# A two-layer graph attention kernel: the order of its first loads, and the second attention of a group done in two halves

## The chip, the cores and the metric

The kernel runs on one core of a Trainium2 chip. Its engines work in parallel, each through its own queue of instructions in order: TensorE (PE; its weight loads are listed apart, as PEld) multiplies, VectorE (DVE) and ScalarE (ACT) do elementwise work and empty TensorE's result banks (PSUM), GpSimd (POOL) does elementwise work on the on-chip memory (SBUF), and SyncE (SP) issues most of the transfers (DMA). ScalarE and GpSimd can issue transfers too. The metric is the time of one execution on the device in microseconds, lower is better.

## The reference

x is 128 graphs of 64 nodes with 512 features, float32; adj is one 64x64 adjacency matrix shared by all graphs. The layer is computed as

```python
h = relu(layernorm(x))                                 # no scale, no shift
# GAT with 4 heads (W_heads: 4 x 512 x 512, a_heads: 4 x 1024), then ELU
Wh = einsum('bnf,hfo->bhno', h, W_heads)
f1, f2 = Wh . a[:, :512], Wh . a[:, 512:]
e = leaky_relu(f1[..., :, None] + f2[..., None, :], 0.01)
attn = softmax(where(adj > 0, e, -1e9), -1)
h1 = elu(attn @ Wh)  # heads side by side: B x N x 2048
# the same once more, with one head: W_out 2048 x 512, a_out
out = elu(gat(h1, W_out, a_out))                       # the "second attention"
y = relu(out @ w1 + b1) @ w2 + b2 + out
result = x + layernorm(y) * gamma + beta
```

ELU is max(v, exp(min(v, 0)) - 1), written below as an exponential on ScalarE and one instruction on VectorE.

## The kernel before

The 8192 rows are 64 tiles of 128 rows (two graphs each), worked in 16 groups of four tiles. Most matrix products are done by a Strassen-like scheme with seven block products in place of eight (`unit`): the products are numbered p = 1 to 7, and go in the order 1, 5, 6, 2, 3, 7, 4. Between them VectorE and ScalarE add blocks in PSUM. The names in the profile: g_a is the first layer's product (x side to heads), g_b the product with W_out, g_c and g_d the two feed-forward products, pa the second attention, hw and pu the first group's own way of doing the first layer.

The front: the loads, and the first products. `ar` holds a_heads in 8 rows of 512; `spread_a` spreads a row of it over all partitions by a product with the identity; `fold` multiplies the weights by it.

```python
X[0] = load(0)                                     # on SyncE's queue
ar = wk.tile([P, O], FP, tag="elu", name="ar", bufs=3)
nc.vector.memset(ar, 0.0)
nc.sync.dma_start(out=ar[0:2 * H], in_=a_heads.rearrange("h (r p) -> (h r) p", p=O))
for t in range(1, G):
    X[t] = load(t)
# ... cut ...
def fetch(m, after=None):
    MT[m] = big.tile([P, KC, O], FP, tag=homes[m], name=f"pw{m}")
    queue = nc.scalar if m == 0 else nc.sync if m < H else nc.gpsimd
    ins = queue.dma_start(out=MT[m], in_=mats[m].rearrange("(k p) o -> p k o", p=P))
    if after is not None:
        behind(ins, after, "not in front of what is needed first")
    return ins
# ... cut ...
for m in range(H):
    fetch(m)
nc.vector.memset(wa, 0.0)
norm1(0)
ab = spread_a(0)                                   # the first products of TensorE (pab)
transpose_h(0)
# ... cut ...
head_w(0, 1)                                       # eight products (hw) and a copy on ScalarE
transpose_h(2)
fold(3, spread_a(3, LAST["pe"]))
weight_sums(1, LAST["nb"])
weight_sums(2, LAST["nb"])
head_w(0, 2)
transpose_h(3)                                     # four transposes (pth), a copy to hT on ScalarE
head_w(0, 3)                                       # needs hT of tile 3
```

The end of a group's first layer. p = 7's result goes through `post`, whose last instruction in PSUM is the addition on line 607; p = 4, which is put off to the next head's second step (`late`), adds into the bank that this addition reads:

```python
def post(what, a, b=None, to=None):                # in project1: g_a
    # ... cut ...
    if b is not None:
        nc.vector.tensor_tensor(to, a, b, ALU.add) # L607
        a = to
    elu(flat(dst), flat(a), f"{what}_{g}_{h}")
# ... cut ...
return [
    s[0], lambda: (s[1](), flush_late()), lambda: (s[2](), next_sums()), s[3], s[4],
    lambda: (s[5](), late.append(s[6])),
]
```

The second attention, and where it stands among the steps of the next group's first layer (four heads of six steps, numbered 0 to 23; the list `stage_e` is spread evenly over them):

```python
def elu(dst, src, name, on_vector=False):
    ex = wk.tile([P, 512], FP, tag="elu", name=f"ex{name}", bufs=3)
    if on_vector:
        nc.vector.tensor_scalar(ex, src, 0.0, None, ALU.min)       # L572
        nc.scalar.activation(ex, ex, AF.Exp)                       # L573
    else:
        nc.scalar.activation(ex, src, AF.Relu, scale=-1.0)         # L575
        nc.scalar.activation(ex, ex, AF.Exp, scale=-1.0)           # L576
    nc.vector.scalar_tensor_tensor(dst, ex, -1.0, src, ALU.add, ALU.max)   # L577

def attend2_all(g):                                # both halves at once, four PSUM banks
    OUT[g] = big.tile([P, G, FO], FP, tag="out", name=f"o{g}")
    pa = [[aux([P, FO], f"pa2_{g}_0_{b}") for b in range(NB)]]
    pa.append([flat(bank(f"pa2_{g}_1_{b}")) for b in range(NB)])
    for finish in [second_attention(g, q, pa[q]) for q in range(2)]:
        finish()

def stage_e(g):
    gap = [lambda: None]
    score = [lambda j=j: scores2(g, j) for j in range(G)]
    return (
        gap + score + [lambda: spread2(g)] + gap * 2 + [lambda: softmax2(g)] + gap * 5
        + [lambda: transpose_weights2(g)] + gap * 5 + [lambda: attend2_all(g)] + gap * 3
    )
```

`aux` gives one of two auxiliary PSUM banks, `bank` one of the six that the block products use. The order of instructions on an engine is the program's, except that a unit's `post` is given priority and instructions that aren't ready may be passed by others when the program is built.

Of the kernel before, what the change touches and what calls it, by code (L numbers as in the profile page):

```python
# [9 lines left out]
FP = mybir.dt.float32  # L10
AF = mybir.ActivationFunctionType
ALU = mybir.AluOpType
# [10 lines left out]
def gat_preln_kernel(  # L23
# [30 lines left out]
    nc = tc.nc  # L54
    P = 128
# [24 lines left out]
    def bank(name):  # L80
        return ps.tile([P, 2, T], FP, tag="mm", name=name)

    def flat(ap):
        return ap.rearrange("p a b -> p (a b)")
# [8 lines left out]
    def aux(shape, name):  # L93
        return ps.tile(shape, FP, tag="aux", name=name, bufs=2)
# [15 lines left out]
    X[0] = load(0)  # L110

    ar = wk.tile([P, O], FP, tag="elu", name="ar", bufs=3)
    nc.vector.memset(ar, 0.0)
    nc.sync.dma_start(out=ar[0:2 * H], in_=a_heads.rearrange("h (r p) -> (h r) p", p=O))
    for t in range(1, G):
        X[t] = load(t)
    aj = const.tile([P, N], mybir.dt.int32, name="aj")
# [45 lines left out]
# [8 lines that stand above are left out]
    def spread_a(m, after=None):  # L171

        ab = []
        for c in range(2):
            pb = flat(bank(f"pab{m}_{c}"))
            r = 2 * m + c
            ins = nc.tensor.matmul(pb, ident[:, r:r + 1].to_broadcast([P, P]), ar, start=True, stop=True)
            if after is not None:
                behind(ins, after, "not in front of it")
            ab.append(pb)  # L180
        return ab

    def fold(m, ab):

        for c in range(2):
            for k in range(KC):
                junk = wk.tile([P, O], FP, tag="t", name=f"jk{c}_{m}_{k}")
                LAST["fold"] = nc.vector.scalar_tensor_tensor(
                    junk, MT[m][:, k, :], 1.0, ab[c], ALU.mult, ALU.mult,
                    accum_out=wa[:, k, c * H + m:c * H + m + 1],  # L190
                )
# [373 lines left out]

    H1, ZSUM = {}, {}

    def elu(dst, src, name, on_vector=False):

        ex = wk.tile([P, 512], FP, tag="elu", name=f"ex{name}", bufs=3)  # L570
        if on_vector:
            nc.vector.tensor_scalar(ex, src, 0.0, None, ALU.min)  # L572
            nc.scalar.activation(ex, ex, AF.Exp)  # L573
        else:
            nc.scalar.activation(ex, src, AF.Relu, scale=-1.0)  # L575
            nc.scalar.activation(ex, ex, AF.Exp, scale=-1.0)  # L576
        nc.vector.scalar_tensor_tensor(dst, ex, -1.0, src, ALU.add, ALU.max)  # L577

    def quadrant(what):
# [130 lines left out]
    def scores2(g, j):  # L710
        if j == 0:
            F2[g] = sm.tile([P, 2, G], FP, tag="f2", name=f"f2_{g}")
        f = F2[g]
        for c in range(2):
            junk = wk.tile([P, FO], FP, tag="elu", name=f"jf{g}_{j}_{c}", bufs=3)
            nc.vector.scalar_tensor_tensor(  # L716
                junk, WH2[g][:, j], 1.0, ao[:, c, :], ALU.mult, ALU.mult,
                accum_out=f[:, c, j:j + 1],
            )
# [20 lines left out]
    def transpose_weights2(g):  # L740
        A = A2.pop(g)
        pt = aux([P, G, P], f"s2pt{g}")
        for j in range(G):
            nc.tensor.transpose(pt[:, j, :], A[:, j].rearrange("p b m -> p (b m)"), ident)
        AT2[g] = wk.tile([P, G, P], FP, tag="hT", name=f"at2_{g}", bufs=4)
        nc.scalar.copy(AT2[g], pt)

    def attend2(g, q):


        if q == 0:
            tag = "out" if g < NG - 1 else "z11"
            OUT[g] = big.tile([P, G, FO], FP, tag=tag, name=f"o{g}")
        second_attention(g, q, [aux([P, FO], f"pa2_{g}_{q}_{b}") for b in range(NB)])()

    def attend2_all(g):

        OUT[g] = big.tile([P, G, FO], FP, tag="out", name=f"o{g}")
        pa = [[aux([P, FO], f"pa2_{g}_0_{b}") for b in range(NB)]]
        pa.append([flat(bank(f"pa2_{g}_1_{b}")) for b in range(NB)])  # L760
        for finish in [second_attention(g, q, pa[q]) for q in range(2)]:
            finish()

    def second_attention(g, q, pa):
        for b in range(NB):
            rows = slice(b * N, (b + 1) * N)
            for c in range(2):
                nc.tensor.matmul(
                    pa[b][c * N:(c + 1) * N], AT2[g][rows, 2 * q + c, rows],
                    WH2[g][rows, 2 * q + c, :], start=True, stop=True, skip_group_check=True,  # L770
                )

        def finish():
            for b in range(NB):
                elu(OUT[g][:, 2 * q + b], pa[b], f"2_{g}_{q}_{b}", b == 1)
        return finish

    def stage_e(g):

        gap = [lambda: None]  # L780
        score = [lambda j=j: scores2(g, j) for j in range(G)]
        return (
            gap + score + [lambda: spread2(g)] + gap * 2 + [lambda: softmax2(g)] + gap * 5
            + [lambda: transpose_weights2(g)] + gap * 5 + [lambda: attend2_all(g)] + gap * 3
        )


# [82 lines left out]


    for m in range(H):
        fetch(m)
    nc.vector.memset(wa, 0.0)
    norm1(0)
    ab = spread_a(0)
# [14 lines left out]
    head_w(0, 1)  # L891
    transpose_h(2)
    fold(3, spread_a(3, LAST["pe"]))
    weight_sums(1, LAST["nb"])
    weight_sums(2, LAST["nb"])
    head_w(0, 2)
    transpose_h(3)
    head_w(0, 3)
    masks()
    head_w(1, 0)  # L900
# [60 lines left out]
    for g in range(NG):  # L961
        if g >= 1:
            side = stage_e(g - 1)
            done, n = 0, 6 * H
            for i in range(n):
                if i % 6 == 0:
                    steps = project1(g, i // 6)
                steps[i % 6]()
                while done * n < (i + 1) * len(side):
                    side[done]()  # L970
                    done += 1
            flush_late()
        attn = attend1(g + 1) if g + 1 < NG else []
        norms, scores, turns = stage_a(g + 2)
        tr, ff, fin = feed_forward(g - 1) if g >= 1 else ([], [], [])
        if g == NG - 1:
            run(project2(g), tr + [nothing] * 6 + ff[:2])
            run(ff[2:], [
                lambda: [scores2(g, j) for j in range(G)], lambda: spread2(g), nothing, nothing,
                lambda: softmax2(g), *[nothing] * 7, lambda: transpose_weights2(g), nothing,  # L980
                *[lambda q=q: attend2(g, q) for q in range(2)], nothing,
            ])
            continue
        early = [lambda: z_sums(g + 1, 0)] if g else []
        first = mix(attn, tr, [nothing] * len(attn))
        if g >= 1:
            first[5:5] = norms[:1]
            first[10:10] = norms[1:]
        if g == 0:
            side = {  # L990
                0: lambda: (attend0(2, 1), turn0(1, 1), project_f(1)),
                1: lambda: (attend0(3, 1), turn0(2, 1)),
                2: lambda: (turn0(3, 1), scores1(1), attn_weights(2), attn_weights(3)),
                5: lambda: weight_sums(M1, LAST["pe"]),
                7: turns1[1],
                8: lambda: fetch(M2, LAST["pe"]),
                9: attn[0],
                10: lambda: (attn[1](), norms[0](), turns1[4]()),
                12: attn[2],
                13: lambda: (attn[3](), norms[1]()),  # L1000
                15: scores[0],
                16: scores[1],
                17: lambda: weight_sums(M2, LAST["pe"]),
                18: scores[3],
                20: scores[5],
                21: scores[7],
                22: lambda: z_sums(g + 1, 0),
                24: turns[1],
                27: lambda: (turns[4](), load_rows()),
            }  # L1010
            for i, fn in enumerate(project2(g)):
                fn()
                side.get(i, nothing)()
        else:
            run(project2(g), first + mix(
                ff[:7] + early + ff[7:12] + fin[:1] + ff[12:13] + fin[1:2] + ff[13:],
                scores + [nothing] * 8,
            ) + mix(fin[2:], [nothing] + turns + [nothing] * 2))
# [32 lines left out]
```

## Time and profile before

| | before |
|---|---|
| time, median of 3 | 2303.92 us (2303.06 to 2304.11) |
| profiled span | 2302.3 us |
| TensorE busy | 2273.8 us, 99% |
| first TensorE instruction | 6.4 us |
| period of a group, from 304.21 to 444.74 us | 140.53 us |
| granted TensorE clock | 0.998 of full speed |

A line of the timeline is: start in us, duration in us, engine, line of the kernel, operation, the tile written <- the tiles read, shape, type and the number of instructions merged into it; in square brackets the idle time of the engine before it, and what ended it. SPq and ACTq are the DMA-issuing queues of SyncE and ScalarE. A line of the waits is: who waited <- for whom: the sum in us, how many times, the longest. Ends of products are modelled, and products overlap in the array, so a product's duration says less than the distance between two starts. One float32 product is listed as two instructions.

### The profile page before, as it was taken

Reading aid. Unit: us, or ns where it says so; the run is one execution under the profiler, and the core shown is the slowest. Engines: PE = TensorE matmul, PEld = TensorE weight load, DVE = VectorE, ACT = ScalarE, POOL = GpSimd, SP = SyncE. Lnnn points to the kernel's source line nnn. Section 1 sums busy time; section 2 is a strip of 40 time slices with the busy share of each in tenths; the row PEclk is TensorE's granted clock in tenths of the full one; section 3 lists DMA queues with packets and bytes.
Section 4 is the critical chain, followed back from the end, with each engine's and each line's share of the span. In section 5 each row is a group of like instructions: output and inputs, shape, how many; then the busy total and the mean of one; then the engine's idle time right before and its main releaser. Section 6 shows DMA issues by size and latency. Waiting matters only on the chain.

```text
span 2302.3 us, 33214 instructions
## 1 busy us (share of the span) xinstructions
PE 2273.8 (99%) x11856; PEld 1894.7 (82%) x11856; DVE 1334.8 (58%) x2259; ACT 894.4 (39%) x1601; POOL 1016.8 (44%) x906
## 2 busy tenths in 40 slices
PE   8999999999999999999999999999999999999997
PEld 4688888888888888888888888888888888888885
DVE  7546554755657555565665646565465565744537
ACT  3535344252442525335253342524425254241512
POOL 7653524444254442634435344352444425533323
PEclk9999999999999999999999999999999999999999
DMA  7553454644545455454544545445454454635543
GB/s 279 197 183 128 147 183 129 182 130 145 177 132 184 137 156 158 135 183 133 168 144 142 183 129 182 130 147 183 129 181 131 149 173 132 183 118 174 156 148 97
DMA packets 255012, 361.15 MB, mean 157 GB/s; under 512 B 23768, under 2 KB 143608, under 8 KB 254848
## 3 DMA queue, kind: packets, MB, share of 16 engines
q1 hardware_dynamic: 249584, 340.90, 47.5%
q0 software_dynamic: 4576, 16.81, 2.0%
q8 instruction: 96, 1.57, 0.3%
q10 hardware_dynamic: 688, 1.31, 0.2%
q14 instruction: 68, 0.56, 0.1%
HBM read 331.66 MB, written 27.26 MB: 156 GB/s over the span
## 4 chain that ended last, share of the span: by engine, by line
PE 90%; DVE 4%; ACT 3%; issue 1%; DMA 0%; POOL 0%; DVEq 0%; SPq 0%; POOLq 0%; ACTq 0%
PE g_b L305 32%; PE g_a L289 27%; PE g_c L289 8%; PE g_d L305 8%; PE pz L547 4%; PE hw L633 2%; PE pto L798 1%; PE pzS L547 1%; PE s1pt L485 1%; PE pth L362 1%; ACT exc L576 1%; PE s1pe L405 1%; PE pf L372 1%; ACT exc L575 1%; DVE o L577 1%
## 5 line engine op out<-in xcount | busy, mean ns | idle before, releaser
L305 PE MATMUL g_b<-w,h 128*128 128x256 f32 x2560 | 593.2, 380 | 0.0
L305 PEld LDWEIGHTS g_b<-w,h 128*128 128x128 f32 x2560 | 481.5, 190 | 64.1 <-issue 2.0
L289 PE MATMUL g_a<-z,w 128*128 128x256 f32 x1440 | 345.0, 383 | 4.2 <-DVE g_a L607 4.2
L289 PE MATMUL g_a<-zs_z,w 128*128 128x256 f32 x1440 | 330.4, 379 | 0.0
L289 PEld LDWEIGHTS g_a<-z,w 128*128 128x128 f32 x1440 | 268.9, 190 | 60.9 <-DVE g_a L607 14.9
L289 PEld LDWEIGHTS g_a<-zs_z,w 128*128 128x128 f32 x1440 | 273.9, 190 | 37.0
L305 PE MATMUL g_b<-w,hS 128*128 128x256 f32 x1024 | 238.2, 379 | 0.0
L575 ACT ACTIVATE exc<-g_a 128x512 f32<-128x512 f32 x240 | 142.7, 595 | 180.6 <-DVE g_a L607 123.9
L305 PEld LDWEIGHTS g_b<-w,hS 128*128 128x128 f32 x1024 | 192.2, 190 | 24.8 <-issue 0.2
L611 POOL TENSOR_TENSOR hS<-hS,h 128x512 f32<-128x512 f32 x60 | 79.6, 1327 | 260.3 <-DVE hS L577 260.3
L577 DVE SCALAR_TENSOR_TENSOR h<-exc,g_a 128x512 f32<-128x512 f32 x180 | 123.2, 684 | 107.7 <-ACT exc L576 107.1
L314 POOL TENSOR_TENSOR zs_z<-zS,z 128x512 f32<-128x512 f32 x60 | 82.5, 1375 | 214.5 <-PE g_a L289 211.2
L692 POOL TENSOR_TENSOR h<-hS,h 128x512 f32<-128x512 f32 x64 | 81.6, 1275 | 165.9 <-PE g_b L305 165.7
L576 ACT ACTIVATE exc<-exc 128x512 f32<-128x512 f32 x240 | 151.2, 630 | 7.5
L692 POOL TENSOR_TENSOR h<-h,h 128x512 f32<-128x512 f32 x64 | 86.8, 1365 | 138.6 <-PE g_b L305 138.6
L489 ACT COPY at<-s1pt 128x512 f32<-128x512 f32 x64 | 34.4, 590 | 272.1 <-PE s1pt L485 272.1
L849 POOL TENSOR_TENSOR xr<-xr,bs 128x512 f32<-128x512 f32 x64 | 97.5, 1528 | 77.0 <-DMA xr<-in_x_dram 43.0
L289 PE MATMUL g_c<-ot,w 128*128 128x256 f32 x512 | 122.8, 383 | 1.7 <-DVE ot L808 1.5
L305 PE MATMUL g_d<-w,rt 128*128 128x256 f32 x512 | 121.8, 380 | 2.0 <-DVE o L841 1.0
L716 DVE SCALAR_TENSOR_TENSOR jf<-wh,ao 128x512 f32<-128x512 f32 x128 | 118.7, 963 | 7.8 <-ACT wh L698 7.6
L289 PE MATMUL g_a<-zS,w 128*128 128x256 f32 x480 | 113.4, 379 | 0.0
L315 POOL TENSOR_TENSOR zs_z<-z,zs_z 128x512 f32<-128x512 f32 x60 | 81.5, 1359 | 70.2 <-PE g_a L289 47.6
(166 smaller groups left out, 3572.0 us busy)
## 6 DMA issues: line engine op xcount, KB each, us to landing
w<-tc SPq DMA_DIRECT2D x624, 256.0 KB, 2.7
w<-in_L_gnn_W_out_dram SPq DMA_DIRECT2D x192, 256.0 KB, 2.7
w<-in_L_gnn_W_heads_dram SPq DMA_DIRECT2D x180, 256.0 KB, 3.3
w<-in_L_gnn_w_dram SPq DMA_DIRECT2D x96, 256.0 KB, 2.8
x<-in_x_dram SPq DMA_DIRECT2D x64, 256.0 KB, 4.6
xr<-in_x_dram SPq DMA_DIRECT2D x128, 128.0 KB, 2.7
out_dram<-o SPq DMA_DIRECT2D x126, 128.0 KB, 2.4
tc<-pt POOLq DMA_DIRECT2D x20, 512.0 KB, 4.3
```

The source lines that it names most:

```text
L289: LAST["pe"] = nc.tensor.matmul(bk[:, o, :], w[:, k, ts(o, P)], a[:, k, :], start=start and o == 0 and k == 0, stop=k == 1, skip_group_che ...
L305: LAST["pe"] = nc.tensor.matmul(bk[:, j, :], a[:, k, ts(j, P)], w[:, k, :], start=start and n == 0, stop=i == len(ms) - 1 and k == 1, skip ...
L314: eng.tensor_tensor(s2, s1, a11, ALU.subtract)
L315: eng.tensor_tensor(s4, a12, s2, ALU.subtract)
L547: nc.tensor.matmul(banks[b][:, c, :].rearrange("p (h n) -> p h n", h=H), src[rows, off + c * P:off + (c + 1) * P], at[rows, b], start=True ...
L575: nc.scalar.activation(ex, src, AF.Relu, scale=-1.0)
L576: nc.scalar.activation(ex, ex, AF.Exp, scale=-1.0)
L577: nc.vector.scalar_tensor_tensor(dst, ex, -1.0, src, ALU.add, ALU.max)
L611: nc.gpsimd.tensor_tensor(dst, dst, H1["22"][:, h], ALU.add)
L692: nc.gpsimd.tensor_tensor(dst[:, h], x0[:, h], x1[:, h], ALU.subtract)
L716: nc.vector.scalar_tensor_tensor(junk, WH2[g][:, j], 1.0, ao[:, c, :], ALU.mult, ALU.mult, accum_out=f[:, c, j:j + 1],)
L849: nc.gpsimd.tensor_tensor(xr, xr, bs, ALU.add)
```

## The change

Three edits aim at the front: the small load of ar is issued by ScalarE ahead of the first head's weights, which are held until the memset of ar is done, so that ar isn't queued behind a megabyte; the last tile's h is transposed before the product of tile 2 rather than after it, so that its copy is done when its own product comes; and group 2's attention weights are transposed one step later in group 0's product with W_out. The fourth takes the second attention in two halves again, at two steps of the next group's first layer, with two banks each, and all its exponentials go the same way (two instructions on ScalarE).

```diff
@@ front
-    nc.vector.memset(ar, 0.0)
-    nc.sync.dma_start(out=ar[0:2 * H], in_=a_heads.rearrange("h (r p) -> (h r) p", p=O))
+    zeros = nc.vector.memset(ar, 0.0)
+    nc.scalar.dma_start(out=ar[0:2 * H], in_=a_heads.rearrange("h (r p) -> (h r) p", p=O))
@@ elu
-    def elu(dst, src, name, on_vector=False):
+    def elu(dst, src, name):
-        if on_vector:
-            nc.vector.tensor_scalar(ex, src, 0.0, None, ALU.min)
-            nc.scalar.activation(ex, ex, AF.Exp)
-        else:
-            nc.scalar.activation(ex, src, AF.Relu, scale=-1.0)
-            nc.scalar.activation(ex, ex, AF.Exp, scale=-1.0)
+        nc.scalar.activation(ex, src, AF.Relu, scale=-1.0)
+        nc.scalar.activation(ex, ex, AF.Exp, scale=-1.0)
@@ attend2 (attend2_all and second_attention are removed, the matmuls stay in attend2)
-        second_attention(g, q, [aux([P, FO], f"pa2_{g}_{q}_{b}") for b in range(NB)])()
+        pa = [aux([P, FO], f"pa2_{g}_{q}_{b}") for b in range(NB)]
         # ... the eight matmuls of this half, cut ...
-        def finish():
-            for b in range(NB):
-                elu(OUT[g][:, 2 * q + b], pa[b], f"2_{g}_{q}_{b}", b == 1)
-        return finish
+        for b in range(NB):
+            elu(OUT[g][:, 2 * q + b], pa[b], f"2_{g}_{q}_{b}")
@@ stage_e
+        attend = [lambda q=q: attend2(g, q) for q in range(2)]
-            + [lambda: transpose_weights2(g)] + gap * 5 + [lambda: attend2_all(g)] + gap * 3
+            + [lambda: transpose_weights2(g)] + gap * 2 + attend[0:1] + gap * 2 + attend[1:2] + gap * 4
@@ front
     for m in range(H):
-        fetch(m)
+        fetch(m, zeros if m == 0 else None)
@@ front
     fold(3, spread_a(3, LAST["pe"]))
+    transpose_h(3)
     weight_sums(1, LAST["nb"])
     weight_sums(2, LAST["nb"])
     head_w(0, 2)
-    transpose_h(3)
     head_w(0, 3)
@@ steps of group 0's product with W_out (turns[1]: transposes of group 2's first weights)
-                24: turns[1],
+                25: turns[1],
```

The list of `stage_e` grows from 24 to 25 entries over the same 24 steps, so that two entries fall on the first step and every later one comes a step earlier: the softmax of the second attention at step 7 (before 8), its transposes at 13 (before 14), and the halves of the attention at 16 and 19 (before both at 20).

More of the change, by code (lines that the diff above doesn't have):

```diff
@@ L753, in attend2 @@
             OUT[g] = big.tile([P, G, FO], FP, tag=tag, name=f"o{g}")
-        second_attention(g, q, [aux([P, FO], f"pa2_{g}_{q}_{b}") for b in range(NB)])()
[L756 to L764, printed above, removed]
+        pa = [aux([P, FO], f"pa2_{g}_{q}_{b}") for b in range(NB)]
         for b in range(NB):
```

## The prediction

> **What bounds the kernel now.** I read the page's shares first, then the waits of TensorE alone, then three stretches of the timeline: the front, the end of one group's first product, and the end of the program.
>
> The page, busy time and the chain that ended last:
>
> ```profile
> PE 2273.8 (99%) x11856; PEld 1894.7 (82%) x11856; DVE 1334.8 (58%) x2259; ACT 894.4 (39%) x1601; POOL 1016.8 (44%) x906
> ...
> PE 90%; DVE 4%; ACT 3%; issue 1%; DMA 0%; POOL 0%; DVEq 0%; SPq 0%; POOLq 0%; ACTq 0%
> ```
>
> TensorE is idle for 2302.3 - 2273.8 = 28.5 us. Removing work from ScalarE, VectorE or GpSimd is worth nothing by itself; only an idle TensorE, or time that TensorE loses within its own stream, can be won. The waits of TensorE name the idle time:
>
> ```profile
> PE pab L177 <- DMA ar<-in_L_gnn_a_heads_dram: 6.4, 1, 6.4
> PE g_a L289 <- DVE g_a L607: 4.2, 15, 0.3
> ...
> PE hw L633 <- ACT hT L364: 0.7, 1, 0.7
> PE s1pt L485 <- DVE s1A L443: 0.4, 1, 0.4
> ```
>
> The first, third and fourth lie in the front, which the change edits by name; the second comes once in each of 15 groups. The timeline of the front, DMA issues and the first products:
>
> ```profile
> 0.72 0.39 SPq L107 DMA_DIRECT2D x<-in_x_dram  x1
> 0.72 0.47 ACTq L166 DMA_DIRECT2D pw<-in_L_gnn_W_heads_dram  x1
> ...
> 0.90 0.48 DVE L113 MEMSET ar<- 128x512 f32 x1 [0.90 <-PEq L1037]
> ...
> 1.41 0.36 SPq L114 DMA_DIRECT2D ar<-in_L_gnn_a_heads_dram  x1
> ...
> 6.43 3.75 PE L177 MATMUL pab<-ar,ident 128*128 128x512 f32 x4 [6.43 <-DMA ar<-in_L_gnn_a_heads_dram]
> ```
>
> The 16 KB of ar are issued at 1.41 and land 4.88 us later (chain of waits), behind 1 MB of weights issued at 0.72. The 256 KB of x0, issued at 0.72, had landed at 3.54 (VectorE's first statistics start there). TensorE only, end of the first product of a group, with the second attention (pa) in it:
>
> ```profile
> 625.87 1.89 PE L289 MATMUL g_a<-zs_z,w 128*128 128x256 f32 x8
> 627.69 1.95 PE L768 MATMUL pa<-wh,at 64*64 64x512 f32 x16
> 629.57 1.99 PE L289 MATMUL g_a<-z,w 128*128 128x256 f32 x8
> 631.40 3.62 PE L289 MATMUL g_a<-zs_z,w 128*128 128x256 f32 x16
> 634.85 1.03 PE L305 MATMUL g_b<-w,h 128*128 128x256 f32 x4
> 636.15 2.00 PE L289 MATMUL g_a<-z,w 128*128 128x256 f32 x8 [0.27 <-DVE g_a L607]
> 637.99 1.03 PE L305 MATMUL g_b<-w,h 128*128 128x256 f32 x4
> ```
>
> Only differences of start times count here: elsewhere eight such products take 1.727 us from start to start (3.45 for 16), so four take 0.864.
>
> **What the skill says.** (1) "TensorEngine Tiling (Array Packing)", Key Properties: "Changing tiling mode (not just tile) drains the TensorE". The trace agrees: before pa the eight products take 627.69 - 625.87 = 1.82, after it 631.40 - 629.57 = 1.83, so entering the 64x64 form costs 0.09 and leaving it 0.10 us; the 128x128 transposes of the weights (s2pt) elsewhere leave the neighbours at 1.73. (2) "DMA: Bandwidth & Descriptors", Queues, rings and completion order: each DMA engine takes turns between the queue rows that have work, and a completion mark lands only after every earlier write of that engine, across queues. The 4.88 us for 16 KB fit that. (3) "TensorE: Matmul & The Clock Gate", Part 1: the array starts at half rate until a window of some 3.4 us has been busy. The first four products take 3.75 us and the next four of that shape 1.88, so this slow start moves with the first product and isn't saved.
>
> **The change part by part.**
>
> *a. ar issued by ScalarE ahead of the first weights.* Nothing is removed; the order is changed. ar still waits for the memset that ends at 0.90 + 0.48 = 1.38, so it is issued at about 1.4, now with the 1 MB behind it and only x0 and x1 (SyncE no longer stops for ar) in another queue. x0 took 3.54 - 0.72 = 2.82 us alone with the weights; 16 KB in a queue of their own should take 2.2 to 2.8. Estimate: landing at 4.0, TensorE starts about 2.4 us sooner. The first weights leave about 1.1 us later (0.72 to 1.85) and now share the engines with x1 to x3. At the 380 GB/s that the front moves, 0.77 MB of x and 1.05 MB of weights take 4.8 us after x0, so they land by 8.4. They are needed at 12.46 - 2.4 = 10.1 by the first hw product, and by the fold, whose other input (the first four products) ends at 4.0 + 3.75 = 7.75. So no new wait: -2.4.
>
> *b. Tile 3's h transposed a product sooner.* Transposes of tile 3 start at 27.07 and four take 0.43, so the next product could start at 27.50; it starts at 28.40, after the copies of hw (0.58) and hT (0.59) on ScalarE. With a product of 3.43 us between, the copy is long done. Its two auxiliary banks come free by then (copy of hw(0,1) ends at 22.26, the transposes would start at 23.6). -0.9.
>
> *c. Group 2's weights transposed one step later.* The transposes at 155.90 had their input ready (DVE ends 155.34). The 0.44 us wait is at the second set, at 162.55, at the end of VectorE's softmax, which is not shortened. The step moves eight products from behind the first set to ahead of it. 0.
>
> *d. The second attention split again,* 15 groups (the sixteenth was split already). Split, each half is eight 64x64 products: in the first tail group 2250.01 to 2251.02, 1.01 us, and in the front 60.24 to 61.26 (pu), 1.02. Together 16 take 629.57 - 627.69 = 1.88. So two halves cost 2 x 1.02 - 1.88 = 0.16 more inside, and one more entry and exit, 0.19: +0.35 a group, x 15 = +5.3.
>
> *e. The closing wait.* Between 634.85 and 636.15 four products (0.864) take 1.30, so 0.44 us are lost, and the wait's restart makes the next eight 1.84 in place of 1.73: 0.55 in all. Its cause is a VectorE that is late. The product g_a at 636.15 accumulates into a bank that VectorE's L607 must have read; that L607 starts at 635.41, though its input was ready at 635.05, because four elus of pa (four exponentials, two of them behind a VectorE minimum) run from 628.9 to 633.75 and hold back the elu of the unit's first block (634.20, after ScalarE came free) and the L607 before it (634.81). With the split, the elus belong to steps 16 and 19 of 24, where now they all belong to step 20, so one half comes four steps sooner and the other one; VectorE also drops two minimums of 0.69 us a group, and ScalarE gains two of 0.60. The end of the program shows the same four-eight-four order without elus in its way:
>
> ```profile
> 2275.35 1.03 PE L305 MATMUL g_d<-w,rt 128*128 128x256 f32 x4
> 2276.30 2.00 PE L289 MATMUL g_c<-ot,w 128*128 128x256 f32 x8
> 2278.13 1.03 PE L305 MATMUL g_d<-w,rt 128*128 128x256 f32 x4
> ```
>
> Four take 0.95 and the eight 1.83: 0.09 + 0.10 = 0.19 lost in place of 0.55. -0.36 a group, x 15 = -5.4.
>
> *f. Tail.* The last group's elus lose two VectorE minimums (0.59 and 0.48 us on the chain at 2252.2 and 2255.5), and its second exponential comes 0.6 later on ScalarE. I take -0.3.
>
> Sum: -2.4 - 0.9 + 0 + 5.3 - 5.4 - 0.3 = -3.7. I add +0.8, because d is certain and e is not: 2303.9 - 2.9 = 2301.0.
>
> **The rivals.** *R1: the closing wait stays,* since the chain product, VectorE, product is inherent and only its queue is shorter; if half of e comes, the time is 2303 to 2304. For it: L607 takes 0.69 us whatever else runs, and four products cover only 0.86. Against it: the tail's 0.19. *R2: the elus on ScalarE make a new wait.* Four relu and exponential pairs of 1.23 us now lie among the posts of heads 2 and 3; the copy (t_a) that lets the seventh product start has 1.9 to 2.2 us to spare there (616.78 to 618.97), and one elu step takes 0.63. If it fails once a group by 0.3 us, +4.5: 2305.5. *R3: the front's gain is lost later,* as the POOL sums or the DMA of group 0 set the pace. Against it: TensorE shows no wait from 28.4 to 162, and the last of the piece loads that wait on those sums is issued at 92.7 against their use at 105. If so, 2304. *R4: the closing wait goes away wholly,* -8.2 in place of -5.4: 2298.
>
> **Range and chances.** The front is worth 2.5 to 4, the groups -3 to +4. The range is 2297.2 to 2304.8. A change of 2% is 46 us; no part reaches it, so within 2% gets 0.99.
>
> **What would show each step.** a: the first TensorE product starts at 3.7 to 4.5 with four products of 3.75 us. b: no wait for hT, and hw products follow on tile 3's transposes without a gap. c: a wait of about 0.4 still at the second set of transposes near 159. d: pa in two stretches of eight, about 1.02 each, neighbours at 1.82. e: the wait for L607 is at most 0.1 us and the period of a group, 140.53 now, stays at 140.3 to 140.7. I am wrong if the period leaves 140.2 to 140.8 (0.3 x 15 = 4.5 us, more than the front gives), if ar lands after 5, or if a new wait for ScalarE shows up fifteen times.

## The result, and the profile after

| | before | after |
|---|---|---|
| time, median of 6 runs each, measured together | 2304.02 us (2303.06 to 2305.11) | 2297.22 us (2295.86 to 2297.82) |
| ratio, with its 95% interval | | 0.997 (0.9957 to 0.9983) |
| profiled span | 2302.3 us | 2293.9 us |
| first TensorE instruction | 6.4 us | 4.5 us |
| period of a group | 140.53 us | 140.37 us |

The change is 6.8 us faster: the direction that was forecast, but more than twice the forecast 2.9, at the very edge of the range. The execution that was profiled after the change was the fastest of its six (2295.86), so the spans differ by 8.4 and not 6.8; the pieces below are therefore also averaged over all traces.

The page of the changed kernel, busy time:

```profile
PE 2273.2 (99%) x11856; PEld 1891.7 (82%) x11856; DVE 1276.5 (56%) x2227; ACT 904.6 (39%) x1633; POOL 1019.9 (44%) x906
```

TensorE is idle for 2293.9 - 2273.2 = 20.7 us in place of 28.5. VectorE has 32 instructions fewer (two minimums in 16 groups) and ScalarE 32 more. VectorE's busy time falls by 1334.8 - 1276.5 = 58 us, more than 32 x 0.69 = 22 us; e3 shows where most of the rest comes from. The waits of TensorE:

```profile
PE pab L177 <- DMA ar<-in_L_gnn_a_heads_dram: 4.5, 1, 4.5
...
PE hw L629 <- DMA pw<-in_L_gnn_W_heads_dram: 0.9, 1, 0.9
```

The fifteenfold wait for L607 and the wait for hT are gone, the first wait is 1.9 us shorter, and there is a new one: the first product hw waits for the first head's weights. The timeline of the front, DMA issues and the first hw:

```profile
1.42 0.59 ACTq L114 DMA_DIRECT2D ar<-in_L_gnn_a_heads_dram  x1
...
2.04 0.44 ACTq L166 DMA_DIRECT2D pw<-in_L_gnn_W_heads_dram  x1
...
2.58 2.42 SPq L166 DMA_DIRECT2D pw<-in_L_gnn_W_heads_dram  x3
...
11.29 3.24 PE L629 MATMUL hw<-pw,hT 128*128 128x512 f32 x7 [0.91 <-DMA pw<-in_L_gnn_W_heads_dram]
```

TensorE starts 1.90 us sooner, but its first product with weights only 12.46 - 11.29 = 1.17 sooner. The pab ahead of it start at 8.50 and are over at 8.50 + 1.72 = 10.22; the weights come at 2.04 + 9.1 = 11.1. In the view of DMA issues the first head's 1 MB takes 9.1 us from issue to landing, before it took 6.5. What the two queues had moved by 11.1 us (packets, MB, share of the 16 DMA engines; q1 is SyncE's queue, q10 ScalarE's):

```profile
q1 hardware_dynamic: 1136, 2.17, 55.8%
q10 hardware_dynamic: 544, 1.07, 26.5%
```

Only 1.05 MB of the 2.17 are the four tiles of x, so about 1.1 MB of what SyncE queues behind them, the later heads' weights first, had gone in between. In before the first weights are there at 0.72 + 6.5 = 7.2, and by then SyncE's queue had moved 0.73 MB.

TensorE only, the end of a group's first layer, at the place that the prediction showed of before:

```profile
616.25 1.09 PE L754 MATMUL pa<-wh,at 64*64 64x512 f32 x8
617.27 2.00 PE L289 MATMUL g_a<-zs_z,w 128*128 128x256 f32 x8
...
632.40 1.03 PE L305 MATMUL g_b<-w,h 128*128 128x256 f32 x4
633.36 2.00 PE L289 MATMUL g_a<-z,w 128*128 128x256 f32 x8
635.19 1.03 PE L305 MATMUL g_b<-w,h 128*128 128x256 f32 x4
```

The eight products ahead of the first half start at 614.43, and the eight behind it are followed by the next at 619.10: the half takes 1.02 (616.25 to 617.27), with 1.82 ahead of it and 1.83 behind it. At the close four products take 0.96 and the eight 1.83. Both are the forecast figures to a hundredth.

So where do the 6.8 us come from? Every trace was cut at the same two products: the first g_a of group 1, and the last group's transposes of out (sixteen pto). From start to start, in us:

| kernel | front | groups | tail | span |
|---|---|---|---|---|
| before | 163.45 | 2093.70 | 45.15 | 2302.3 |
| after | 161.38 | 2091.01 | 41.51 | 2293.9 |
| mean of the traces without / with this part of the change | 163.55 / 162.39 | 2093.56 / 2091.17 | 44.46 / 41.69 | |
| difference of the means | -1.2 | -2.4 | -2.8 | -6.4 |

The means: front, 7 and 4 traces; groups, 5 (with the whole attention at step 20 and the minimums) and 4; tail, 7 (with the two VectorE minimums) and 7, all from the experiments below. The tails with the minimums form two sets: before, e4 and e9 take 44.62 to 45.15 us, and e1, e3, e5 and e12 43.95 to 44.21 (see e2). The forecast had -3.3 for the front, -0.1 for the groups and -0.3 for the tail. The error in the front is hidden in the total by the two others, of opposite sign.

### The profile page after: what moved, and what is told of

It is laid out like the page before. It is cut to its first block, busy times and chain, and to the rows that moved or that the text cites. A ratio compares the mean times of both kernels' runs of the same rounds, so it can differ in the third digit from the quotient of the medians.

```text
span 2293.9 us, 33254 instructions
## 1 busy us (share of the span) xinstructions
PE 2273.2 (99%) x11856; PEld 1891.7 (82%) x11856; DVE 1276.5 (56%) x2227; ACT 904.6 (39%) x1633; POOL 1019.9 (44%) x906
## 5 line engine op out<-in xcount | busy, mean ns | idle before, releaser
L289 PE MATMUL g_a<-zs_z,w 128*128 128x256 f32 x1440 | 336.0, 381 | 0.0
L607 POOL TENSOR_TENSOR hS<-hS,h 128x512 f32<-128x512 f32 x60 | 78.0, 1300 | 359.7 <-DVE hS L573 359.7
L314 POOL TENSOR_TENSOR zs_z<-zS,z 128x512 f32<-128x512 f32 x60 | 85.2, 1419 | 134.8 <-PE g_a L289 131.6
L305 PEld LDWEIGHTS g_d<-w,rt 128*128 128x128 f32 x512 | 97.0, 190 | 16.9 <-DVE o L825 2.7
L712 DVE SCALAR_TENSOR_TENSOR jf<-wh,ao 128x512 f32<-128x512 f32 x128 | 96.7, 792 | 24.1 <-ACT wh L694 23.8
```

What stands on the lines that cost most here:

```text
L289: LAST["pe"] = nc.tensor.matmul(bk[:, o, :], w[:, k, ts(o, P)], a[:, k, :], start=start and o == 0 and k == 0, stop=k == 1, skip_group_che ...
L305: LAST["pe"] = nc.tensor.matmul(bk[:, j, :], a[:, k, ts(j, P)], w[:, k, :], start=start and n == 0, stop=i == len(ms) - 1 and k == 1, skip ...
L314: eng.tensor_tensor(s2, s1, a11, ALU.subtract)
L607: nc.gpsimd.tensor_tensor(dst, dst, H1["22"][:, h], ALU.add)
L712: nc.vector.scalar_tensor_tensor(junk, WH2[g][:, j], 1.0, ao[:, c, :], ALU.mult, ALU.mult, accum_out=f[:, c, j:j + 1],)
```

## The experiments

The kernel before was run again with each batch; its median was 2303.75 to 2303.94. "Before" and "after" in an edit say which kernel it starts from.

### e1: the front alone

Before, with the three front edits (ar on ScalarE's queue, tile 3's h sooner, turns[1] at step 25) and nothing else.

> The kernel before with the three front edits alone. Theory (the front gives what its trace shows, no more): TensorE starts at 4.5, waits 0.9 us for the first weights, and the first g_a product of group 1 stands at 161.4 in place of 163.45; nothing after it moves, period of a group 140.53, time 2302.0. Rival A (the front also moves the tail, through the state of the queues): time 2299 or less with the period unchanged. Rival B (gain lost later): 2304.

Measured: 2302.20 us, ratio 0.9994 (0.9986 to 1.0003): 1.7 us, not certain to be more than nothing. The trace has the first pab at 4.34 and the first hw only at 12.44, after 1.94 us of idle TensorE; the weights, issued at 2.05, land 10.2 us later, at 12.25. From the first hw to the first g_a of group 1 it takes 162.53 - 12.44 = 150.09 us, where before took 163.45 - 12.46 = 150.99. That is step b, 0.90, and what TensorE won by its early start it loses again at the first weights. The tail is shorter than before's, 43.95 us in place of 45.15, as rival A has it; but e3, e5 and e12, with the front of before, have 44.12 to 44.21, so it isn't the front that shortens it.

### e2: only the last group's minimums removed

Before, with

```diff
-    elu(OUT[g][:, 2 * q + b], pa[b], f"2_{g}_{q}_{b}", b == 1)
+    elu(OUT[g][:, 2 * q + b], pa[b], f"2_{g}_{q}_{b}", b == 1 and g < NG - 1)
```

> The kernel before, with the last group's four elus alone on ScalarE (no VectorE minimum there). Theory: on GpSimd the small n2rs operation of the tail comes ahead of the four long additions of b2s, so the VectorE queue isn't held and the g_c product that waited 2.07 us for nothing visible starts 2 us sooner: time 2300 to 2301.5, all before the last group unchanged. Rival (the tail's gain in the trace is a chance of one run, or my own estimate of 0.3 holds): 2303.5 to 2304.

Measured: 2300.78 us, ratio 0.9986 (0.998 to 0.9993). Two instructions of 0.69 us in the last group are worth 3.1 us; the groups stay at 2093.67. The timelines of the tail say how. Before:

```profile
2257.84 5.85 POOL L800 TENSOR_TENSOR o<-o,b2s 128x512 f32<-128x512 f32 x4 [1.94 <-PE pto L798]
...
2260.82 1.75 DVE L808 TENSOR_TENSOR ot<-ot 128x512 f32<-128x512 f32 x1
...
2262.62 1.99 PE L289 MATMUL g_c<-ot,w 128*128 128x256 f32 x8 [1.54 <-DVE ot L808]
...
2264.24 1.74 DVE L853 SCALAR_TENSOR_TENSOR o<-o,n2rs,xr 128x512 f32<-128x512 f32 x1 [1.67 <-POOL n2rs L334]
...
2265.90 0.68 DVE L314 TENSOR_TENSOR zs_o<-ot,ot 128x512 f32<-128x512 f32 x1
...
2266.68 3.61 PE L289 MATMUL g_c<-zs_o,w 128*128 128x256 f32 x8 [2.07 <-issue]
```

In e2:

```profile
2258.04 6.41 POOL L800 TENSOR_TENSOR o<-o,b2s 128x512 f32<-128x512 f32 x4 [1.18 <-PE pto L798]
2258.16 1.69 DVE L853 SCALAR_TENSOR_TENSOR o<-o,n2rs,xr 128x512 f32<-128x512 f32 x1
...
2260.98 0.67 DVE L808 TENSOR_TENSOR ot<-ot 128x512 f32<-128x512 f32 x1
...
2261.72 1.60 DVE L314 TENSOR_TENSOR zs_o<-ot,ot 128x512 f32<-128x512 f32 x1
...
2263.53 1.89 PE L289 MATMUL g_c<-zs_o,w 128*128 128x256 f32 x8
```

Read L853, the scaling of a finished row. Without the minimums VectorE reaches that tile's statistics sooner, its n2rs (the small GpSimd operation that makes the scale of a row from its variance) goes through GpSimd ahead of the four long additions of b2s, and L853 stands at 2258.16, ahead of L808. With them n2rs comes at 2263.65, behind the additions, and L853 waits in VectorE's queue in front of L314, for which TensorE waits (the 2.07 that the trace calls "issue": the product starts when L314 is done). From the first product of this stage to the third TensorE takes 2266.68 - 2259.19 = 7.49 us before and 2263.53 - 2259.12 = 4.41 in e2.

This difference is not yet the gain. In e2 TensorE waits 1.06 us for t_c later on, and before loses more behind the two waits, because its granted TensorE clock (0.50, the third number from the right) is halved there:

```profile
2267.00:2270.00 3.00, 3.00 (x8) 2.38 (x8) 2.65 (x7) 0.00 (x0) 0.93 (x1) 0.50 0.77 190
```

The eight products at 2266.68 take 3.41 us up to the next start, 2270.09; in e1, at full clock, the same ones take 1.80. The traces of e4 and e9 have such a stretch too, those of e1, e3 and e5, with the same two waits ahead of it, have none; why is not shown. Against the 41.69 us of the tails without the minimums, those with them take 2.4 us more at full clock (mean of e1, e3, e5 and e12: 44.1) and 3.2 more with the stretch (44.9).

### e3: the list a step earlier, nothing else

Before, with a 25th entry in the list, so that the softmax of the second attention comes at step 7 and the whole attention at step 19:

```diff
-    gap * 5 + [lambda: attend2_all(g)] + gap * 3
+    gap * 5 + [lambda: attend2_all(g)] + gap * 4
```

> The kernel before with one more empty entry at the end of the second attention's list, so that its softmax, transposes and the undivided attention each come one step sooner (7, 13 and 19); nothing is split. Theory: the hidden wait at the second head's closing (0.18 us, softmax in VectorE's way) goes, and the closing wait at the fourth head shrinks as its elus are a step sooner: period 140.0 to 140.35, time 2296 to 2301. Rival A (it is the split, not the step, that gains): period 140.53, time 2304. Rival B: only the closing wait or only the hidden one goes: 140.17 or 140.35.

Measured: 2304.50 us, ratio 1.0004 (0.9995 to 1.0012). The period is 140.60 us, but not because nothing happened. First, a loss that no view of waits had listed for TensorE. The timeline of before, VectorE, GpSimd and TensorE, at the closing product of the second head (611.52):

```profile
608.24 1.27 POOL L316 TENSOR_TENSOR zs_z<-z,zs_z 128x512 f32<-128x512 f32 x1 [0.39 <-PE g_a L289]
608.32 1.21 DVE L453 TENSOR_TENSOR s2rb<-blkones,s2r 128x8 f32<-128x8 f32 x1
...
610.77 0.69 DVE L607 TENSOR_TENSOR g_a<-g_a,s_a 128x512 f32<-128x512 f32 x1
...
611.51 1.59 PEld L289 LDWEIGHTS g_a<-z,w 128*128 128x128 f32 x8 [0.31 <-DVE g_a L607]
611.52 1.99 PE L289 MATMUL g_a<-z,w 128*128 128x256 f32 x8
```

The product ahead of it starts at 609.72, the one behind it at 613.35, distances of 1.80 and 1.83 where 1.727 is usual: 0.18 us lost per group. The product at 611.52 carries no idle time in brackets, because the modelled end of the one before reaches beyond its start; only the weight load names L607. L607 stands in VectorE's queue behind the softmax of the second attention, and in it a multiply of 128 x 8 numbers, s2rb, took 1.21 us: until GpSimd's addition was over (608.24 + 1.27 = 609.51). The same in after:

```profile
603.10 0.17 DVE L453 TENSOR_TENSOR s2rb<-blkones,s2r 128x8 f32<-128x8 f32 x1
...
603.94 1.27 POOL L315 TENSOR_TENSOR zs_z<-z,zs_z 128x512 f32<-128x512 f32 x1 [0.86 <-PE g_a L289]
```

a step sooner, between two GpSimd additions, it takes 0.17. The Trainium skill, "SBUF — State Buffer", Who interferes with whom, states that a VectorE instruction with two SBUF inputs contends with a GpSimd instruction that reads SBUF, since its second input comes through a shared interface, and that the shared port pair is an exclusive lock. The traces agree: s2rb takes 1.21 in before, e1, e4 and e5, where it falls into that addition, and 0.17 in after, e3 and e6, where it doesn't; the 0.18 of TensorE is lost in the first four and not in the last three. Had s2rb taken 0.17, L607 would have been done 1.04 us sooner, at 610.42, and nothing would have waited; this last step is worked out, no run removed the collision alone. A second instruction of the same softmax, L435, takes 1.37 us in before and 0.42 in after beside another GpSimd addition; 15 x (1.04 + 0.95) = 30 us are most of the 36 us of VectorE's busy time that the minimums don't explain.

Second, e3 pays for it. TensorE only, the end of the group:

```profile
631.28 3.92 PE L289 MATMUL g_a<-zs_z,w 128*128 128x256 f32 x16
```

At step 19 the four elus hold up one product inside the sixteen (the next starts at 635.04, 3.76 later and not 3.45), and still the closing one, which starts at 636.28 (1.24 later and not 0.95). A step is not better for being earlier; it has to miss the posts of the products.

### e4: split, but at the old steps

Before, split in halves at steps 17 and 20, with ScalarE's elus in groups 0 to 14; the list keeps its 24 entries, the softmax its step 8, and the tail its minimums.

```diff
-    gap * 5 + [lambda: attend2_all(g)] + gap * 3
+    gap * 2 + attend[0:1] + gap * 2 + attend[1:2] + gap * 3
```

> The kernel before with the attention in two halves as in the changed kernel, and all-ScalarE elus in groups 0 to 14, but the list kept at 24 entries, so that the softmax stays at step 8 and the halves come at 17 and 20; tail and front as before. Theory: the split costs 0.35, the closing wait falls from 0.55 to 0.2 to 0.4, the hidden wait of 0.18 stays: period 140.5 to 140.7, time 2303.5 to 2306. Rival (the split by itself makes the period): 140.37, time 2301.5.

Measured: 2304.33 us, ratio 1.0 (0.9992 to 1.0008), period 140.55 us. TensorE only, the second head:

```profile
610.32 1.89 PE L289 MATMUL g_a<-zS,w 128*128 128x256 f32 x8
612.12 1.99 PE L289 MATMUL g_a<-z,w 128*128 128x256 f32 x8
613.95 1.89 PE L289 MATMUL g_a<-zs_z,w 128*128 128x256 f32 x8
```

The close, at 635.81, 636.77 and 638.60, loses 0.19 (0.96, 1.83), as in after; the hidden loss of the second head is there again (1.80, 1.83). So the split and the close cancel, +0.35 and -0.36 a group, as steps d and e had it, and the 0.18 a group by which after is shorter still (140.55 to 140.37) is the shift of the list.

### e5: only the exponentials, at step 20

Before, with `b == 1 and g == NG - 1`: all elus of groups 0 to 14 on ScalarE, the attention whole and at its old step.

> The kernel before, the undivided attention left at step 20, with all elus of groups 0 to 14 on ScalarE (the last group keeps its VectorE minimums). It tells whether the VectorE minimum or the place of the elus makes the closing wait. Theory (place: all four elus still stand ahead of the closing posts, and ScalarE now needs eight instructions in a row): the closing wait stays or grows, period 140.5 to 140.8, time 2303.5 to 2308. Rival (the minimum holds VectorE): the closing loses 0.2 in place of 0.55, period 140.2, time 2299.

Measured: 2308.13 us, ratio 1.0017 (1.0011 to 1.0024), period 140.82 us. The closing wait grows; from the waits of TensorE:

```profile
PE g_a L289 <- DVE g_a L607: 8.5, 15, 0.6
```

It was 4.2 us in all. So taking two minimums from VectorE doesn't shorten this wait, it lengthens it; that ScalarE, with two more instructions, gives the elus back later is the likely reason. With all exponentials on ScalarE the wait is there at step 20 and gone at the places of e4, after and e6: what shortens it is the place of the elus, not the engine. Whether those places would do as well with the minimums kept, no run shows; e3, at step 19, keeps 0.2 of the wait.

### e6: the attention whole, at step 16

After, with both halves back together, all exponentials on ScalarE:

```diff
-    gap * 2 + attend[0:1] + gap * 2 + attend[1:2] + gap * 4
+    gap * 2 + [lambda: attend2_all(g)] + gap * 7
```

> The changed kernel with the second attention of a group undivided again, but at step 16, eleven products ahead of the closing posts. Theory: one entry and exit of the 64x64 form is saved (0.35 us a group by the measured 1.02, 1.88, 0.09 and 0.10), and no post is held: period 140.02, time 2292. Rival (four elus in a row hold some post wherever they stand, as at step 19): 140.3 to 140.6, time 2296 to 2301.

Measured: 2292.37 us, ratio 0.9949 (0.9936 to 0.9961), period 140.01 us. The sixteen products of pa start at 616.68 and the next at 618.56: they take 1.88 in place of 2 x 1.02, one entry and exit is saved, and the close stays at 0.95 and 1.83 (632.48, 633.43, 635.26): the groups take 2085.80 us, 5.4 less than the 2091.17 of the split, or 0.36 a group. The split was never needed; its cost is step d, and its use is that of an earlier step.

### e7: the later heads' weights held back

After, with the loads of heads 1 to 3 issued only after the first tile's statistics:

```diff
     for m in range(H):
-        fetch(m, zeros if m == 0 else None)
+        if m == 0:
+            fetch(0, zeros)
+    # after spread_a(0):
+    for m in range(1, H):
+        fetch(m, LAST["nb"])
```

> The changed kernel with the loads of heads 1 to 3's weights (3 MB on SyncE's queue) held until tile 0's mean is done on GpSimd, near 6 us. Theory (the first weights land at 11 and not at 8.4 because 3 MB more share the engines with them): they land by 9.5, TensorE's wait for them goes, and the first hw product stands at 10.2 to 10.5 in place of 11.3; first g_a product of group 1 near 160.5, time 2296.2. Rival (the later weights of heads 1 to 3 are then late, or the queue is shared by x alone): a new wait at the fold or at the first product of head 1, time 2297 to 2299.

Measured: 2297.41 us, ratio 0.997 (0.9959 to 0.9982). It says little on its question: SyncE's queue sent four pieces of W_out and the two loads of ao instead, 6 x 256 KB, so the first weights still shared the engines; hw started at 11.72 after a wait of 0.3. What came true is the rival: the fold of the later heads ends at 34.96 us and not at 30.80 as in after, the products that read it wait, and from the first hw to the first g_a of group 1 it takes 151.07 us in place of 150.09.

### e11: the first head's weights in two halves

After, with the load of the first head cut in two: one half on ScalarE's queue behind ar, the other on SyncE's behind x1 and ahead of x2 and x3.

```diff
-    for t in range(1, G):
-        X[t] = load(t)
+    X[1] = load(1)
     # ... cut; in fetch, for m == 0:
+    ins = queue.dma_start(out=MT[m][:, 0:2], in_=src[:, 0:2])
+    nc.sync.dma_start(out=MT[m][:, 2:4], in_=src[:, 2:4])
+    for t in range(2, G):
+        X[t] = load(t)
```

> The changed kernel with the first head's weights loaded in two halves, one on ScalarE's queue behind ar, one on SyncE's queue behind x1 and ahead of x2 and x3. Theory (the weights' landing, at 11.3 to 12.8 in the runs so far, sets the first hw product and eats what the earlier ar wins): both halves land by 9.5, the first hw product stands at 10.2 to 10.5, the first g_a product of group 1 at 160.0 to 160.5, time 2295.5 to 2296.5. Rival (the landing is bound by all that is in flight, not by the order): 11.3 to 12.8 again, time 2297.

Measured: 2296.51 us, ratio 0.9968 (0.9956 to 0.9981). Products of the front:

```profile
8.68 1.88 PE L183 MATMUL pab<-ar,ident 128*128 128x512 f32 x4
10.40 3.19 PE L635 MATMUL hw<-pw,hT 128*128 128x512 f32 x7
```

hw follows pab without a gap, and the first g_a of group 1 starts at 160.93, 1.5 us ahead of the mean with the front edits. The halves land at about 10.2 us (1.64 + 8.4 and 2.04 + 8.2). So it was the landing of the first weights that took the gain of the early start; that 3 MB of later weights delay it fits the 1.1 MB that had gone in between in after, but no run took them away. The order has a price: x2 and x3 come later, the second hw waits 0.22 us for hT, and from the first hw to g_a it takes 150.53 us in place of 150.09. The median is 0.7 us below after's; the two intervals overlap.

### e8: turns[1] back at step 24

After, with `24: turns[1]` in place of 25.

> The changed kernel with group 2's attention weights transposed at step 24 again. Theory (the step does nothing: the wait of 0.4 us is at the second set): time 2297.0 to 2297.6, the same wait of 0.4 to 0.5 us at the second set of transposes. Rival (the later step is needed with the earlier front): a wait at the first set as well, time 2297.7 to 2298.5.

Measured: 2297.70 us, ratio 0.9974 (0.9962 to 0.9985). The wait of 0.45 is at the second set of transposes, 161.87, and none is at the first. In after it is 0.43, at 160.48, also at the second. Step c does nothing that can be seen.

### e9 and e12: is it GpSimd's order in the tail?

e9: before, with the last group's four additions of b2s written later in the program.

> The kernel before with the last group's four GpSimd additions of b2s put behind the finishing steps of group 14, so that the small n2rs operation isn't queued behind them; the VectorE minimums stay. Theory (the tail's gain comes from GpSimd's order): the 2.07 us wait of the g_c product goes, time 2300.5 to 2302. Rival (it is the VectorE minimums' 1.2 us on the chain, or the wait is for something else): 2303 to 2304.

Measured: 2303.84 us, ratio 0.9999 (0.9991 to 1.0007). The additions still went ahead of the second n2rs in GpSimd's queue, so the run tested nothing. e12 therefore makes them wait for that n2rs:

```diff
+    # last group: the four additions run behind the second n2rs
+    [behind(add(), LAST["n2rs"], "small one first") for add in held]
```

> The kernel before, with only the order on GpSimd changed at one place: the last group's four additions of b2s (5.85 us) wait for the second small n2rs operation, which stood behind them; VectorE's minimums stay, and every other engine keeps its order. Theory (the tail's gain is this order): VectorE's L853 no longer waits 1.67 us for n2rs, the g_c product behind it loses its 2.07 us wait, time 2301 to 2302. Rival (the two minimums on VectorE's chain make the gain): 2303.5 to 2304.5.

Measured: 2303.73 us, ratio 0.9999 (0.9991 to 1.0007). Timeline of its tail, where n2rs now runs at 2258.60 and the additions from 2259.68:

```profile
2259.78 1.76 DVE L853 SCALAR_TENSOR_TENSOR o<-o,n2rs,xr 128x512 f32<-128x512 f32 x1
...
2261.46 1.75 DVE L314 TENSOR_TENSOR zs_o<-ot,ot 128x512 f32<-128x512 f32 x1
```

L853's wait for n2rs is gone, and L808 takes 0.69 us at 2259.17. Yet L853 still stands between L808 and L314, L853 and L314 take 1.75 beside the additions, and TensorE waits 1.34 us for L314 and later 1.98 for t_c. From the first product of this stage to the third it takes 4.96 us, near e2's 4.41, but the later waits take that gain back. The tail is 44.18 us, within the 43.95 to 45.15 of all kernels with the minimums; without them it is 41.46 to 41.92. The theory that GpSimd's order alone is the cause falls. What the runs show is that the two minimums cost 2.4 us at full clock and 2.8 in the mean of all traces; that they do so by pushing L853 behind L808 is read from the traces, and how much of it is L853's place and how much its collision with GpSimd stays open.

### e14: the version that beats both

e6 and e11 together: after, with the whole attention at step 16 and the first weights in two halves.

> The changed kernel with the undivided attention at step 16 and the first weights in two halves. Theory: both gains add up, 2297.2 - 4.9 - 1.3 = 2291.0; period 140.01. Rival (the halves do nothing): 2292.4.

Measured: 2290.97 us (2290.51 to 2291.29), ratio 0.9944 (0.9931 to 0.9956): 12.8 us faster than before and 6.3 faster than after. The wait for the first weights is gone from its trace, and its three pieces are 161.28, 2085.70 and 41.92 us. Yet its first hw starts at 11.24 and not at 10.40 as in e11: the second four pab ahead of it take 2.42 us from start to start, in e11 1.72.

## Why the prediction was right and wrong

The forecast that this is a change of a few us, within 2%, and faster, held; the size failed, because two terms of the sum were far too small and one far too large.

- *f, the tail: the term that was most mis-sized.* Forecast -0.3; over the traces -2.8, and alone in e2 -3.1. The step counted the two minimums as 0.59 and 0.48 us on one chain and gave most of it back to ScalarE. It left out what stands behind them in VectorE's queue: without them L853 leaves ahead of L808 and no longer stands between L808 and L314, the two that TensorE waits for. GpSimd's order, which changes along with it, doesn't do it alone (e12). 2.4 us are there at full clock; the rest is the half-clock stretch that three of the seven traces with the minimums have. How the 2.4 divide between L853's place and its collisions with GpSimd is open.
- *The groups: a term that was missing.* d and e came out as forecast, +0.35 and -0.36 (e4: 140.55 us when both act alone). But the list also shifts the softmax by a step, which the description of the change names and for which the prediction had no term. It removes 0.18 us a group, 2.4 to 2.7 us in all. The loss stood in the trace of before, as start distances of 1.80 and 1.83; the prediction looked only at the end of the first product, and for the rest took the list of waits, in which it doesn't appear.
- *e's reason was half right.* It gave two causes for the closing wait, the place of the elus and VectorE's minimums. e5 shows that removing the minimums alone makes it worse (0.57), e4 and e6 that the place settles it once they are removed.
- *a, ar first: right up to its last sentence.* TensorE starts at 4.3 to 4.5 us, at the late end of the forecast 3.7 to 4.5. "They land by 8.4 ... so no new wait" was wrong: the first weights landed at 11.1 in after and at 12.3 to 12.7 in e1, e8 and e6, and TensorE waited 0.9 to 2.6 us for them. The step shared the engines among x and these weights only, and left out the 3 MB of later weights that SyncE queues from 2.58 us on, right behind x: about 1.1 MB had moved behind x by 11.1 us, which at the 380 GB/s of the forecast is 2.9 us, about the distance from 8.4 to 11.1 (an estimate). The forecast quoted the Trainium skill, "DMA: Bandwidth & Descriptors", Queues, rings and completion order, on taking turns between queues, for the 16 KB of ar, which in before stood in SyncE's queue beside the megabyte in ScalarE's and not behind it; the same sentence applied to the 1 MB, and e11 agrees with it. Of -2.4 next to nothing remains: over the traces with the edits (after, e1, e6, e8) TensorE starts 2.03 us sooner than over the seven without, and waits 2.03 us for the weights. The first hw starts at 12.29 in the mean and not at 12.53; these 0.24 us are a difference of the slow first products (last section). In this pair of traces it is 1.17.
- *b* came out at 0.90, *c* at nothing, as forecast.
- *The +0.8 of caution* was put against e, the term that held.

Of the rivals, R1 (the wait stays) and R2 (a new wait for ScalarE; none recurs in the groups) didn't come. R3 (the front's gain is lost later) came for step a: a transfer takes it, but already at the first hw, not in group 0's later work. R4's 2298 is the closest figure, but by another cause: the close still loses its 0.19.

## What to carry to other kernels

On an engine that is 99% busy, read the distances between starts, and compare equal stretches: a loss of 0.18 us that recurs 15 times weighs as much as a wait at the head of the list, and needn't be listed at all. When a small load is moved ahead of a large one, work out next who waits for the large one, with everything that is queued beside it counted. Before work is split to make room for other work, try it whole at another step; and where VectorE combines two operands in SBUF, see what GpSimd does at that moment. And before the difference of two traces is put down to an edit, compare the granted clock in the stretch: here it made eight products of the tail take 1.6 us longer.

## What the runs showed of the hardware that was not expected

A VectorE multiply of 128 x 8 numbers took 1.21 us or 0.17 us, as GpSimd was or wasn't in the middle of an addition, and additions of 128 x 512 in the tail 1.75 or 0.67. Without an edit of the kernel's front, the start of the first hw moved between 11.83 and 13.08 us from one kernel to the next, so 1 us in the front is within what a single trace can show by chance. Nothing waits there: from the first pab to the first hw these traces take between 5.37 us (e12) and 6.64 (e4) for the same products, which run slow for a shorter or longer time before they come to full speed (the second four of pab take 1.72 us from start to start in e12, 2.24 in e4). In the tail, the granted clock fell to 0.50 for 3.4 us in three of seven traces, as said at e2.
